# Splitting each store's 16 KB run per partition into two runs of 8 KB, in a per-sample 128x128 matmul with residual

## The chip, the cores and the metric

One NeuronCore of a Trainium2 chip runs the program. The metric is device microseconds of one execution, as the median of several executions. Inputs and outputs lie in HBM; all of x (67.1 MB) is read once and an output of the same size is written once.

## What is computed

There are 128 samples of x, each 128 channels by 1024 times in float32, eight weight matrices of 128x128, and an index per sample that names its matrix.

```
def reference(x, itok_B_0_7, L0_cond_weights):       # (128,128,1024) f32, (128,) int32, (8,128,128) f32
    w = weights[subjects]                            # subjects = itok_B_0_7
    out = jnp.einsum('bct,bcd->bdt', x, w)
    return x + out
```

## The kernel before, in words

**Tiling.** Four samples make a group (G = 2 samples to a pair, H = 2 pairs to a group), so there are NT = 32 groups. A group lives in one of SLOTS = 12 tiles in SBUF, `xs[k]`, of 128 partitions by 4 samples by 1024 floats: 16 KB in each partition, 2.1 MB in all. The result is added in place, so the same tile is loaded, computed on and stored from.

**Loads.** SyncE's queue (SP) issues all loads, in the order of the samples, one DMA for each sample (`load`, line 121). On the HBM side a sample is described as 16 pieces of 8 lines (`rearrange("(a r) t -> a (r t)", r=ROWS)`, ROWS = 8), each 32 KB without a gap; on the SBUF side as 128 partitions of 4 KB. Each of the 16 DMA engines takes one 32 KB piece and fills eight partitions with it. From the thirteenth group on SP first waits until the slot's former group has been stored (lines 165 to 167: `s_first` once, then `s_pair[k][H - 1]` at the count that `emptied` gives). So loads can run ahead of stores by twelve groups at most, 25.2 MB.

**Compute.** For each pair of samples GpSimd (POOL) copies the two weight matrices that the index names (line 196), waiting for the pair's load. TensorE multiplies (line 206, eight matmuls of 128x512 to a pair) into PSUM, and VectorE adds PSUM and the tile into the tile (line 217).

**Stores.** ScalarE's queue (ACT) issues the stores (`store`, line 130) as soon as VectorE is done with their samples (line 222). Groups 1 to 30 have one store each, of all four samples. Group 0 has two stores of two samples each. The last group has one of two samples and one of one sample, and the very last sample goes by an ordinary DMA at the end. On the HBM side a store is described as 128 lines (d) by so many samples (g) of 4 KB each; on the SBUF side, by line 136, as one run for each partition, 16 KB long where there are four samples, 8 KB where there are two. Each of the 16 DMA engines takes eight partitions.

Loads and stores thus stand on two queues, which the same 16 DMA engines serve. In the profile the queue of the loads is q1 and that of the stores q10. Each load or store also ends with one transfer of 4 bytes on every engine that counts up its semaphore; these stand in the profile's DMA records among the ones under 512 B.

Of the kernel before, what the change touches and what calls it, by code (L numbers as in the profile page):

```python
# [30 lines left out]
G = 2  # L31
# [18 lines left out]
def transfer(nc, engine, out, in_):  # L50

    later, nc._always_lower_symbolic_ap = nc._always_lower_symbolic_ap, False
    ins, outs = engine.lower_ap_dma(in_), engine.lower_ap_dma(out)
    nc._always_lower_symbolic_ap = later
    return engine.add_instruction(  # L57
        mybir.InstDMACopy(
            name=nc.get_next_instruction_name(),
            engine=engine.engine,  # L60
            ins=ins,
            outs=outs,
            mode="Copy",
            cce_op=ALU.bypass,
            queue=QUEUES[engine.engine],
        )
    )
# [3 lines left out]
def kernel(  # L71
# [12 lines left out]
    def sbuf(name, *shape, dtype=F32):  # L84
        return ctx.enter_context(nc.sbuf_tensor(name, list(shape), dtype)).ap()
# [7 lines left out]
    xs = [sbuf(f"x{i}", C, H * G, T) for i in range(SLOTS)]  # L93
# [36 lines left out]
    def store(i, q0, q1):  # L130
        k, b = i % SLOTS, i * H * G
        transfer(
            nc,
            nc.scalar,
            out[b + q0 : b + q1].rearrange("g d t -> d g t"),
            xs[k][:, q0:q1, :].rearrange("d (o g) t -> d o (g t)", o=1),
        ).then_inc(s_first if i == 0 and q1 == G else s_pair[k][(q1 - 1) // G], DMA)

    with tc.tile_critical():  # L139
# [22 lines left out]
        for i in range(NT):  # L162
            k = i % SLOTS
# [8 lines left out]
        for j in range(NT * H):  # L172
            i, q0, q1 = j // H, j % H * G, (j % H + 1) * G
            k = i % SLOTS
# [46 lines left out]
            if i == 0 or q1 == H * G or i == NT - 1:  # L221
                nc.scalar.wait_ge(s_added, j + 1)
                store(i, q0 if i in (0, NT - 1) else 0, q1 - (b == B - 1))
# [42 lines left out]
```

## Time and profile before

| what | value |
|---|---|
| median of three runs (lowest to highest) | 347.12 us (345.59 to 358.03) |
| the profiled execution | 345.59 us, span 343.8 us |
| TensorE matmul busy | 243.7 us, 71% of the span |
| VectorE busy | 147.8 us, 43% |
| GpSimd busy | 34.0 us, 10% |
| read from HBM, written to HBM | 67.63 MB, 67.11 MB |
| mean rate over the span | 392 GB/s |
| loads (q1): share of the 16 DMA engines' span | 51.4% |
| stores (q10): the same | 46.7% |

The span is the time from the first to the last instruction that the profile shows; 1.8 us of the execution's own time lie around it. In the profile's DMA tables a queue's row gives its packets, the MB that they moved and the time that they took, as a share of 16 engines' time in the stretch that was asked for. So a share of 50% in a stretch of 10 us is 80 us of DMA engine time. Tables by stretch count the span from its start.

### The profile page before, as it was taken

Reading aid. Unit: us, or ns where it says so; the run is one execution under the profiler, and the core shown is the slowest. Engines: PE = TensorE matmul, PEld = TensorE weight load, DVE = VectorE, ACT = ScalarE, POOL = GpSimd, SP = SyncE. Lnnn points to the kernel's source line nnn. Section 1 sums busy time; section 2 is a strip of 40 time slices with the busy share of each in tenths; the row PEclk is TensorE's granted clock in tenths of the full one; section 3 lists DMA queues with packets and bytes.
Section 4 is the critical chain, followed back from the end, with each engine's and each line's share of the span. In section 5 each row is a group of like instructions: output and inputs, shape, how many; then the busy total and the mean of one; then the engine's idle time right before and its main releaser. Section 6 shows DMA issues by size and latency. Waiting matters only on the chain.

```text
span 343.8 us, 1606 instructions
## 1 busy us (share of the span) xinstructions
PE 243.7 (71%) x518; PEld 94.5 (27%) x518; DVE 147.8 (43%) x68; POOL 34.0 (10%) x132
## 2 busy tenths in 40 slices
PE   6886866877777887777887777887777877775000
PEld 2332322333222333222333232233322322231000
DVE  1164353445544445544445554445553455345000
POOL 1011011011111011111011111101111011010000
PEclk9899999999999999999999999999999999999555
DMA  7999999999999999999999999999999999999993
GB/s 198 236 260 296 283 356 425 417 431 426 423 425 427 427 427 427 417 426 425 431 421 425 431 422 429 423 411 410 417 416 414 404 416 419 429 410 427 427 420 132
DMA packets 10186, 134.85 MB, mean 392 GB/s; under 512 B 2625, under 2 KB 3650, under 8 KB 3906
## 3 DMA queue, kind: packets, MB, share of 16 engines
q1 hardware_dynamic: 5136, 67.64, 51.4%
q10 hardware_dynamic: 5042, 67.11, 46.7%
q8 instruction: 4, 0.07, 0.1%
q14 instruction: 4, 0.03, 0.0%
HBM read 67.63 MB, written 67.11 MB: 392 GB/s over the span
## 4 chain that ended last, share of the span: by engine, by line
PE 36%; issue 26%; DVE 21%; POOL 4%; DMA 2%; POOLq 1%; SPq 0%
PE ps L206 36%; DVE x L217 21%; POOL w L196 4%; DMA x<-in_x_dram 2%; POOLq L196 1%; POOLq L185 1%; SPq L57 0%; SPq L161 0%; POOLq L139 0%; SPq L262 0%; SPq L139 0%
## 5 line engine op out<-in xcount | busy, mean ns | idle before, releaser
L206 PE MATMUL ps<-x,w 128*128 128x512 f32 x512 | 238.3, 609 | 69.3 <-POOL w L196 66.2
L217 DVE TENSOR_TENSOR x<-ps,x 128x2048 f32<-128x2048 f32 x64 | 146.6, 2291 | 167.4 <-PE ps L206 167.4
L206 PEld LDWEIGHTS ps<-x,w 128*128 128x128 f32 x512 | 92.7, 191 | 215.6 <-POOL w L196 117.5
L196 POOL COPY w<-w_all 128x128 f32 x128 | 33.8, 293 | 276.7 <-DMA x<-in_x_dram 271.2
L146 PE MATMUL ps<-zeros 128*128 128x512 f32 x6 | 5.5, 1084 | 1.7 <-DVE zeros L143 1.7
L146 PEld LDWEIGHTS ps<-zeros 128*128 128x128 f32 x6 | 1.8, 326 | 3.8 <-issue 2.1
L143 DVE MEMSET zeros<- 128x512 f32 x1 | 0.5, 485 | 1.1 <-SPq L139 1.1
L153 DVE TENSOR_SCALAR near<-given 1x128 int32<-1x128 int32 x1 | 0.2, 216 | 0.6 <-DMA given<-in_itok_B_dram 0.6
L157 DVE CUSTOM_DVE_ANT_0 index<-near,wrap 1x256 uint16<-1x256 uint16 x1 | 0.3, 278 | 0.0
L155 DVE TENSOR_SCALAR wrap<-near 1x128 int32<-1x128 int32 x1 | 0.2, 215 | 0.0
L253 POOL MEMSET const-float32-0.0<- 128x1 f32 x1 | 0.1, 98 | 0.2 <-issue 0.2
L253 POOL MEMSET const-bfloat16-1.0<- 128x1 bf16 x1 | 0.1, 101 | 0.0
L253 POOL MEMSET const-uint8-127<- 128x1 uint8 x1 | 0.1, 101 | 0.0
L253 POOL MEMSET const-float32-1.0<- 128x1 f32 x1 | 0.1, 98 | 0.0
## 6 DMA issues: line engine op xcount, KB each, us to landing
x<-in_x_dram SPq DMA_DIRECT2D x128, 512.0 KB, 36.5
out_dram<-x ACTq DMA_DIRECT2D x30, 2048.0 KB, 40.0
out_dram<-x ACTq DMA_DIRECT2D x3, 1024.0 KB, 25.7
out_dram<-x ACTq DMA_DIRECT2D x2, 512.0 KB, 21.2
w_all<-in_L_cond_weights_dram SPq DMA_DIRECT2D x1, 512.0 KB, 4.8
given<-in_itok_B_dram ACTq DMA_DIRECT2D x1, 0.5 KB
```

The costliest lines, as they stand in the source:

```text
L143: nc.vector.memset(zeros, 0.0).then_inc(s_zeros, 1)
L146: nc.tensor.matmul(ps[P_SLOTS - 1][:, G - 1, :N], zeros[:, :D], zeros, start=True, stop=True)
L153: nc.vector.tensor_scalar(near, given, -S, S - 1, ALU.max, ALU.min).then_inc(s_index, 1)
L155: nc.vector.tensor_scalar(wrap, near, 0, S, ALU.is_lt, ALU.mult).then_inc(s_index, 1)
L157: nc.vector.tensor_tensor(index, near, wrap, ALU.add).then_inc(s_index, 1)
L185: _, subject = nc.values_load_multi_w_load_instructions(index[0:1, b : b + R], engines=[mybir.EngineType.Pool], min_val=0, max_val=S - 1, ...
L196: copy = nc.gpsimd.tensor_copy(ws[b % W_SLOTS], w_all[:, bass.ds(subject[b % R], 1), :])
L206: mm = nc.tensor.matmul(p[:, q % G, t : t + N], ws[(i * H * G + q) % W_SLOTS][:, 0, :], xs[k][:, q, t : t + N], start=True, stop=True,)
L217: nc.vector.tensor_tensor(mine, p, mine, ALU.add).then_inc(s_added, 1)
L253: nc = _bacc.Bacc("TRN2", target_bir_lowering=False, num_devices=1)
```

## The change

One line of `store` changes, in how the SBUF side of a store is described. With four samples, a partition's 16 KB are now two runs of 8 KB (two samples each), where they were one run of 16 KB. For stores of two samples `min(G, q1 - q0)` is 2 and for one of one sample it is 1, which gives one run as before: the stores of groups 0 and 31 stay as they were. The bytes, the HBM side, the loads, the order on every queue and all semaphores are the same.

```
--- before.py
+++ after.py
@@ -133,7 +133,7 @@
             nc,
             nc.scalar,
             out[b + q0 : b + q1].rearrange("g d t -> d g t"),
-            xs[k][:, q0:q1, :].rearrange("d (o g) t -> d o (g t)", o=1),
+            xs[k][:, q0:q1, :].rearrange("d (o g) t -> d o (g t)", g=min(G, q1 - q0)),
         ).then_inc(s_first if i == 0 and q1 == G else s_pair[k][(q1 - 1) // G], DMA)
 
     with tc.tile_critical():
```

More of the change, by code (lines that the diff above doesn't have):

```diff
@@ L135, in store @@
             out[b + q0 : b + q1].rearrange("g d t -> d g t"),
-            xs[k][:, q0:q1, :].rearrange("d (o g) t -> d o (g t)", o=1),
+            xs[k][:, q0:q1, :].rearrange("d (o g) t -> d o (g t)", g=min(G, q1 - q0)),
         ).then_inc(s_first if i == 0 and q1 == G else s_pair[k][(q1 - 1) // G], DMA)
```

## The prediction

> **What bounds the kernel now.** I read the page's busy slices first. The lines are the mean busy share of the 16 DMA engines and what they moved, in 40 slices of 8.6 us; below them the row of GpSimd's weight copies, whose idle time says what compute waits for.
>
> ```profile
> DMA  7999999999999999999999999999999999999993
> GB/s 198 236 260 296 283 356 425 417 431 426 423 425 427 427 427 427 417 426 425 431 421 425 431 422 429 423 411 410 417 416 414 404 416 419 429 410 427 427 420 132
> ...
> L196 POOL COPY w<-w_all 128x128 f32 x128 | 33.8, 293 | 276.7 <-DMA x<-in_x_dram 271.2
> ```
>
> The DMA engines are busy from end to end, and compute waits 271.2 us for loads: the kernel is bound by its transfers. But busy engines don't always move the same. In the first five slices they are as busy as later and move 198 to 296 GB/s, where later they move about 425. So I asked for four stretches (busy time of PE, PEld, DVE, POOL, then granted clock, DMA share, GB/s):
>
> ```profile
> 8.00:24.00 16.00, 12.53 (x24) 4.98 (x24) 5.05 (x3) 0.84 (x4) 0.89 1.00 234
> 28.00:44.00 16.00, 11.10 (x24) 4.31 (x24) 7.72 (x4) 1.59 (x6) 1.00 1.00 301
> 60.00:300.00 240.00, 188.55 (x408) 73.25 (x408) 115.95 (x51) 26.47 (x100) 1.00 1.01 422
> 312.00:335.00 23.00, 2.71 (x7) 0.93 (x5) 2.90 (x2) 0.00 (x0) 0.63 1.00 424
> ```
>
> Loads alone (8 to 24 us) run at 234 GB/s and stores alone (312 to 335) at 424. From 28 to 44 us loads run beside the two stores of group 0, which are already in runs of 8 KB: 301 GB/s. The first 16 KB run stands in the trace's transfer records at 46 us, and from there on the rate is 422. So the trace of before holds a stretch of what the change makes of the rest. The DMA queues' rows (packets, MB, share of 16 engines) of 28 to 44, of 60 to 300, of 335 to 338, of 0 to 46 and of 306 to 344 us, in this order:
>
> ```profile
> q1 hardware_dynamic: 201, 3.31, 72.1%
> q10 hardware_dynamic: 200, 1.51, 28.3%
> ...
> q1 hardware_dynamic: 3265, 53.52, 53.4%
> q10 hardware_dynamic: 3265, 47.58, 47.0%
> ...
> q10 hardware_dynamic: 192, 0.89, 71.9%
> ...
> q1 hardware_dynamic: 1596, 9.90, 82.9%
> q10 hardware_dynamic: 284, 2.10, 13.9%
> ...
> q10 hardware_dynamic: 1218, 13.40, 83.4%
> ```
>
> Look at the MB. From 60 to 300 us loads and stores stand as 53.52 to 47.58, which is 1.125. From 28 to 44 they stand as 2.19. And both queues have the same number of packets in both stretches. That is what turns taken one transfer at a time give. A load is two transfers on each engine (32 KB and its semaphore). A store of four samples is nine (eight of 16 KB and its semaphore), so nine turns against 4.5 loads: 4.5 x 32 / (8 x 16) = 1.125. With group 0's runs of 8 KB it is 4.5 x 32 / (8 x 8) = 2.25.
>
> What a load costs also differs. From 28 to 44 us, 72.1% of 256 us of engine time over 3.31 MB is 1828 ns for 32 KB, and a run of 8 KB costs 393 ns. From 60 to 300 it is 1256 ns, and a run of 16 KB costs 621 ns.
>
> **What the change does.** *More pieces.* Thirty stores have 256 runs in place of 128: 7680 of 8 KB for 3840 of 16 KB. Stores alone cost 618 ns for 16 KB (23 us x 16 engines over 9.76 MB) and 318 ns for 8 KB (71.9% of 48 us over 0.89 MB, with some of 4 KB in it). So 9 ns more a piece at most, 9 x 7680 / 16 = 4 us; nothing at least. I take 2.
>
> *Turns.* A store now takes 17 turns against 8.5 loads: loads to stores are 8.5 x 32 / (16 x 8) = 2.125, so of all bytes 68% are loads and 32% stores, as long as both queues hold work. Whether they do is the next step. A load lands 36.5 us (median) after its issue, some 8 MB at the 223 GB/s of loads from 60 to 300 us, so its queue is deep. And among the waits of SP the only ones of note for stores are those of line 229, at the program's end; the slot waits of lines 165 and 167 don't stand there. First the page's row of issues, then the row of SP's waits (total, times, longest):
>
> ```profile
> x<-in_x_dram SPq DMA_DIRECT2D x128, 512.0 KB, 36.5
> ```
>
> ```profile
> SPq L229 <- DMA out_dram<-x: 18.3, 3, 9.8
> ```
>
> So slots are no limit now. With 68 to 32 they become one. Three stages follow.
>
> *Stage 1, from 46 us until twelve slots are full.* At 46 us 9.90 MB less 0.52 of weights are loaded, 9.38, and 2.10 stored: 7.3 MB in slots, of 25.2. I take the rate from the row that has this mix, 301 GB/s. Loads gain 36% of it on stores, 108 GB/s, so the other 17.9 MB fill in 165 us: to 211 us. By then 43.2 MB are loaded and 18.0 stored; before, that stretch ran at 421.
>
> *Stage 2, loads held by slots.* The load queue runs empty, a store ends, and SP issues one group's loads to all engines at once. The 23.9 MB left to load go one for one with stores, 47.8 MB. How fast, no row says directly. If the one-to-one mean decides, it is 422 GB/s as from 60 to 300: 113 us. If each burst goes as from 28 to 44, an engine needs 4 x (1828 + 2 x 393) + 8 x 318 = 13,000 ns for its share of 4.19 MB, 323 GB/s: 148 us. Half of the runs go beside loads, half don't, so I take the middle, 372 GB/s: 128 us, to 339 us.
>
> *Stage 3, stores alone.* 67.1 - 18.0 - 23.9 = 25.2 MB at 424 GB/s are 59 us, and the tail stays: 37.8 us from 306 on less 13.40 MB at 424 leave 6 us.
>
> Sum: 211 + 128 + 59 + 6 + 2 = 406, and 1.8 outside the span: 408, against the profiled execution's 345.6 (the median of the runs, 347.1, is 0.4% above). With stage 2's ends: 393 to 428.
>
> Compute is no cover and no cost: in the chain of waits TensorE's eight matmuls of a pair take 3.71 us, and pairs will come more slowly. ACT issues as many DMAs as before; if more pieces hold it, only later stores stand behind, and those wait for engines anyway. SP's waits on slots, nearly free now, become long, with nothing behind them but loads that have no room.
>
> **Two rules beside the rows.** The trace's turns are of one transfer, by the 1.125 and 2.19. The Trainium skill (DMA: Bandwidth & Descriptors, Queues, rings and completion order) says that an engine drains a whole packet, about 9 to 17 descriptors typically, before it switches. By that both halves of a run could stay in one turn and the time would be about 347. And loads alone move 234 GB/s here. The same page (Bandwidth, Measured) has 425 GB/s for a 16 MB load; with that, a mix with more loads would cost nothing, again about 347. The rows of this case speak against both.
>
> **Rivals.** *Only reading is capped.* The 301 GB/s could be a start-up of the mix, while the true limit is the 234 GB/s that loads reach alone. Then stage 1 runs at 234 / 0.68 = 344, fills 17.9 MB at 124 in 144 us, to 190 us; stage 2 takes 113 us at full rate, or 131 with bursts at 2240 ns a load (4 x 2240 + 8 x 318). With 59, 6, 2 and 1.8: 372 to 390. For it: a plain limit. Against: from 28 to 44 us loads moved only 3.31 MB / 16 us = 207.
>
> *Not slower: the first 46 us are slow for their own sake.* Loads may be slow early because all engines start in step, or for the place of the first samples, and the 8 KB runs are there by chance. Then a load keeps its 1256 ns, stage 1 runs near 421, loads only get ahead, stores alone end it at 424, and 2 us are added: 347.6, 345 to 350. It decides if 32 KB beside two runs of 8 KB moves at full rate, which asks reads of 0.68 x 421 = 286 GB/s; from 60 to 300 they were 223. For it: nothing else differs so sharply in time as start and rest. Against: the change of rate falls on the first 16 KB runs.
>
> *The change does nothing.* The two runs adjoin in SBUF and could be merged into 16 KB again: 346. Against it: the built program describes the side as 128 x 2 x 2048 floats.
>
> Faster is hardly to be had: from 46 us on all bytes move at 421 of 424.
>
> **The numbers.** The three stages at mixed rates: 52%, 393 to 428, at 408. Reading capped: 24%, 372 to 390. Slow start only: 18%; merged: 3%. Something that I don't see makes it faster: 3%. A measurement here tells about 2% from no change. So faster 0.03, same 0.21, slower 0.76. Leaving out the no-change cases would leave out more than 2 in 10, so the range runs from 346 to 428; that of the likeliest case is 393 to 428.
>
> **What would show it.** About twice the packets of over 4 KB on q10; loads to stores near 2.1 in MB and near 300 GB/s from 46 to about 210 us; SP held on stores from then on; the last load landing well before the end, with nearly 60 us of stores alone. Wrong if the rate from 60 us on is again 420 (slow start), or the packets are as many as now (merged).

## The result, and the profile after

| | before | changed |
|---|---|---|
| median, us (six executions each) | 357.18 (345.59 to 360.32) | 399.84 (383.28 to 415.60) |
| ratio | | 1.1075, 95% interval 1.0963 to 1.1186 |
| the profiled execution, us | 345.59 (span 343.8) | 383.88 (span 382.1) |
| transfers on the stores' queue (q10) | 5042 | 8882 |
| last load landed, us of the span | 309 | 328 |

The change makes the kernel 11% slower. Executions of both kernels scatter by 4 to 8%, so the ratio is taken from the quickest ones of each (383.28 and 383.88 us against 345.59 and 347.12); what goes with the scatter comes out below.

The page of the changed kernel shows the busy share of the DMA engines and what they moved in 40 slices (now of 9.6 us), the two queues, and how long a load takes from issue to landing:

```profile
DMA  9999999999999999999999999999999999999996
GB/s 220 220 248 281 301 305 295 300 302 316 334 402 421 424 423 425 410 347 356 318 295 366 346 413 314 362 362 352 386 357 411 372 407 357 385 427 426 425 425 281
...
q1 hardware_dynamic: 5136, 67.64, 54.7%
q10 hardware_dynamic: 8882, 67.11, 44.6%
...
x<-in_x_dram SPq DMA_DIRECT2D x128, 512.0 KB, 15.9
```

The DMA engines are as busy as before, but after the start, where loads stand alone, four stretches follow each other: some 300 GB/s up to about 95 us, then 420 to 425 up to about 155, then an uneven stretch of 295 to 413, then 425 with stores alone. The same four, asked for as stretches (columns: busy time of PE, PEld, DVE, POOL, granted clock, DMA share, GB/s):

```profile
46.00:90.00 44.00, 31.81 (x67) 12.48 (x66) 18.54 (x9) 4.24 (x16) 0.96 1.01 302
110.00:155.00 45.00, 44.59 (x99) 17.62 (x98) 27.90 (x13) 6.88 (x26) 1.00 1.01 423
165.00:330.00 165.00, 115.39 (x224) 46.49 (x224) 64.15 (x28) 15.26 (x58) 0.87 1.01 359
335.00:370.00 35.00, 0.00 (x0) 0.00 (x0) 1.80 (x1) 0.00 (x0) 0.53 1.01 426
```

The queues' rows for 46 to 90 us, for 110 to 155 and for 340 to 370:

```profile
q1 hardware_dynamic: 551, 8.98, 70.9%
q10 hardware_dynamic: 553, 4.27, 29.6%
...
q1 hardware_dynamic: 788, 12.94, 68.4%
q10 hardware_dynamic: 787, 6.06, 32.4%
...
q10 hardware_dynamic: 1664, 12.80, 101.4%
```

Loads to stores are 8.98 to 4.27 = 2.10 and 12.94 to 6.06 = 2.14, with equal numbers of transfers on both queues. So the mix is the same in both stretches, and yet one runs at 302 and the other at 423 GB/s. Per 32 KB piece of a load that is 70.9% of 704 us of engine time over 274 pieces, 1.82 us, against 68.4% of 720 us over 395, 1.25 us. SP's waits for slots show that these were full. The row is what SP waited for at the loads' line, in total, times, longest:

```profile
SPq L57 <- DMA out_dram<-x: 155.2, 16, 14.3
```

Before, there was no such row. That a load now lands 15.9 us after its issue and not 36.5 says the same: its queue is often empty.

### The profile page after: what moved, and what is told of

The parts are those of the page before. It is cut to its first block, busy times and chain, and to the rows that moved or that the text cites. A ratio compares the mean times of both kernels' runs of the same rounds, so it can differ in the third digit from the quotient of the medians.

```text
span 382.1 us, 1606 instructions
## 1 busy us (share of the span) xinstructions
PE 256.4 (67%) x518; PEld 102.4 (27%) x518; DVE 147.8 (39%) x68; POOL 34.0 (9%) x132
## 3 DMA queue, kind: packets, MB, share of 16 engines
q10 hardware_dynamic: 8882, 67.11, 44.6%
## 4 chain that ended last, share of the span: by engine, by line
PE 46%; issue 23%; DVE 13%; POOL 3%; DMA 2%; POOLq 1%; SPq 0%
PE ps L206 46%; DVE x L217 13%; POOL w L196 3%; DMA x<-in_x_dram 2%; POOLq L196 1%; SPq L57 0%; SPq L161 0%; POOLq L185 0%; SPq L262 0%; SPq L139 0%
## 5 line engine op out<-in xcount | busy, mean ns | idle before, releaser
L206 PE MATMUL ps<-x,w 128*128 128x512 f32 x512 | 251.5, 643 | 76.4 <-POOL w L196 72.1
L206 PEld LDWEIGHTS ps<-x,w 128*128 128x128 f32 x512 | 100.5, 205 | 227.5 <-POOL w L196 116.7
## 6 DMA issues: line engine op xcount, KB each, us to landing
x<-in_x_dram SPq DMA_DIRECT2D x128, 512.0 KB, 15.9
```

Of the source, the lines that this page charges most:

```text
L206: mm = nc.tensor.matmul(p[:, q % G, t : t + N], ws[(i * H * G + q) % W_SLOTS][:, 0, :], xs[k][:, q, t : t + N], start=True, stop=True,)
```

## The experiments

The prediction took 301 GB/s for a property of the mix. The trace of the changed kernel already speaks against that. From there two theories stood: **A**, runs of 8 KB beside loads are slow in themselves, and something else ended it; **B**, slowness belongs to the 32 KB loads when they stand alone, and a mix heavy in loads keeps it where an even mix ends it. Each experiment is one profiled execution unless a median is given. With 32 KB loads two executions of one kernel can lie 20 to 32 us apart, so what follows rests on the rates within one execution, and a single span is rough.

### 1. The same mix after another start

```
-            xs[k][:, q0:q1, :].rearrange("d (o g) t -> d o (g t)", g=min(G, q1 - q0)),
+            xs[k][:, q0:q1, :].rearrange("d (o g) t -> d o (g t)", g=(q1 - q0) if i <= 3 else min(G, q1 - q0)),
```

> Runs of 16 KB for groups 0 to 3 as in the kernel before, 8 KB from group 4 on. Theory A (8 KB runs beside loads always give about 300 GB/s): 420 GB/s from about 46 to 76 us, then about 300 until the slots are full; span near 400 us. Theory B (the slow state stems from the start, where loads stand alone; a mix of 8 KB runs only fails to end it): 420 GB/s goes on after 76 us with loads to stores near 2.1, until the slots are full at about 190 us, then about 370; span near 357 us.

Span 362.4 us. Stretches of this kernel:

```profile
28.00:44.00 16.00, 12.03 (x27) 4.76 (x28) 8.33 (x4) 1.60 (x6) 1.00 1.03 310
60.00:80.00 20.00, 16.76 (x34) 6.71 (x35) 8.66 (x4) 2.13 (x8) 0.91 1.00 420
85.00:170.00 85.00, 84.78 (x188) 33.69 (x187) 53.12 (x24) 12.27 (x46) 1.00 1.01 423
190.00:310.00 120.00, 86.79 (x170) 34.77 (x169) 48.13 (x21) 11.21 (x42) 0.87 1.01 359
```

From 85 to 170 us the runs are of 8 KB again, and the queues' rows for this stretch give 24.35 to 11.54 MB, 2.11: the mix of the slow stretch, at 423 GB/s for 85 us. Theory A falls. Three groups of 16 KB runs end the slow loads (60 to 80 us), and 8 KB runs don't bring it back. The bursts at the end (359) stay.

### 2. Runs of 16 KB where the slots are full

```
-            xs[k][:, q0:q1, :].rearrange("d (o g) t -> d o (g t)", g=min(G, q1 - q0)),
+            xs[k][:, q0:q1, :].rearrange("d (o g) t -> d o (g t)", g=(q1 - q0) if i >= 8 else min(G, q1 - q0)),
```

> Runs of 8 KB for groups 1 to 7, 16 KB from group 8 on, which meets full slots. If the second stage's loss stems from turns (loads 2.1 to 1, so they come in bursts), it is gone: about 420 GB/s from the end of the first stage (some 165 to 210 us) on, span near 360 us. If it stems from full slots as such, about 370 GB/s stays and the span is near 380 us.

Span 384.2 us:

```profile
46.00:120.00 74.00, 52.63 (x115) 20.51 (x114) 32.43 (x15) 7.41 (x28) 1.00 1.00 292
...
210.00:330.00 120.00, 86.09 (x179) 33.57 (x177) 50.42 (x22) 11.65 (x44) 0.96 1.00 384
```

The expectation that turns make the second stage slow missed: with nearly even turns and full slots the rate is 384, somewhat over the 359 of 8 KB runs but far from 420. By its span this is the rival's case, full slots as such; experiment 6 shows that it isn't that either. The first, slow stretch, whose runs are those of the changed kernel, lasted longer here, to about 129 us: its length differs from execution to execution.

### 3. Loads alone, in pieces of 32, 16 and 4 KB

Three kernels that load all of x and leave out compute and all stores but the last sample's, the first with ROWS = 8 and then

```
-ROWS = 8
+ROWS = 4
```

and ROWS = 1 in the third.

> Leaves out compute and all stores but the last sample: the loads of x alone, in 32 KB pieces, each group waiting for its slot's former load. If loads alone are slow by themselves: 234 GB/s to the end, span near 295 us. If slow for the start of the program only: rate rises to about 425 after some 50 to 100 us, span near 190 to 220 us.

> The same, but each sample is read as 128 pieces of 4 KB, one to a partition. If the 32 KB piece makes loads slow: well above 234 GB/s, 350 to 425, span 165 to 200 us. If reading by 16 engines at these addresses is slow in any pieces: 234 again, span near 295 us.

> As the run of loads alone (compute and all stores but the last sample left out), with 64 pieces of 16 KB a sample in place of 32 KB (231 GB/s) and 4 KB (410 GB/s). If loads slow down with the piece's size gradually: between, 300 to 380 GB/s, span 185 to 230 us. If only pieces over 16 KB are slow: about 410 to 425, span near 170 us.

Stretches within the steady part, columns: length, busy time of POOL, granted clock, DMA share, GB/s. First 32 KB:

```profile
20.00:280.00 260.00, 0.00 (x0) 1.00 1.01 235
```

then 16 KB:

```profile
20.00:150.00 130.00, 0.00 (x0) 1.00 1.01 409
```

and 4 KB:

```profile
20.00:150.00 130.00, 0.00 (x0) 1.00 1.03 410
```

The spans are 296.0, 173.6 and 173.5 us. It is neither the program's start nor reading by 16 engines as such: the same bytes into the same partitions move at 409 or 410 GB/s in pieces of 16 or 4 KB and at 235 in pieces of 32 KB, to the end. Of the two cases written down for 16 KB the second holds: the loss comes in one step between 16 and 32 KB. ROWS sets more than the size, though. A load gives each engine one piece of 32 KB, two of 16 KB or eight of 4 KB, and a piece fills eight, four or one partitions. No run keeps these apart, for instance by giving each engine two pieces of 32 KB in one load; "pieces of 32 KB" below stands for loads cut in this way.

### 4. Loads alone, 32 KB after a fast start

```
-            x[i * H * G + q].rearrange("(a r) t -> a (r t)", r=ROWS),
+            x[i * H * G + q].rearrange("(a r) t -> a (r t)", r=1 if i < 4 else ROWS),
```

> Loads alone (compute and all stores but the last sample left out), 4 KB pieces for groups 0 to 3, 32 KB from then on. If 32 KB pieces are slow only where all engines start them together: over 400 GB/s throughout, span near 172 us. If they are slow where they stand alone: 410 GB/s for 8 MB, then about 231; span near 280 us.

```profile
8.00:20.00 12.00, 0.00 (x0) 1.00 1.03 413
30.00:250.00 220.00, 0.00 (x0) 1.00 1.01 240
```

Span 275.1 us. So 32 KB loads that stand alone are slow even when they follow a fast stretch. It isn't the common start of all engines.

### 5. The changed kernel and the kernel before with that fast start

The same edit of `load`, in the changed kernel:

> The changed kernel with the loads of groups 0 to 3 in 4 KB pieces, 32 KB from group 4 on. If the slow state stems from 32 KB pieces that stand alone at the start: about 410 GB/s from some 5 us on and no stretch near 300 before the slots are full; then bursts at about 370; span 335 to 350 us. If 32 KB pieces beside 8 KB runs fall into it by themselves: about 300 GB/s from group 4's loads (some 25 us) on, span 370 us or more.

Span 355.4 us:

```profile
46.00:140.00 94.00, 92.21 (x205) 36.66 (x203) 58.17 (x26) 13.68 (x52) 1.00 1.01 421
155.00:290.00 135.00, 90.70 (x181) 35.92 (x182) 52.60 (x23) 11.64 (x44) 0.90 1.00 341
```

The 32 KB loads meet stores from their first moment on and run at 421 GB/s, at a mix of 26.91 to 12.63 MB, 2.13. What is left is the second stage, at 341. The same in the kernel before, timed:

> The kernel before with the same start: groups 0 to 3 in 4 KB pieces. The first 46 us of before move 12 MB, which at 410 GB/s take 29 us after a start of 4: if the slow start is just this, 13 us less than before, ratio near 0.965. If the loads that come sooner only wait for compute and slots, ratio 0.99 to 1.0.

Median 341.90 us (341.31 to 350.09, five executions) beside 357.11 (342.79 to 361.92, seven). The profiled one took 347.94:

```profile
8.00:30.00 22.00, 21.81 (x51) 9.62 (x52) 12.36 (x6) 2.67 (x10) 1.00 1.03 420
36.00:54.00 18.00, 15.07 (x25) 6.28 (x26) 4.69 (x3) 2.13 (x8) 0.74 0.98 340
...
310.00:346.00 36.00, 11.10 (x24) 4.31 (x24) 8.11 (x4) 1.12 (x5) 0.76 0.53 222
```

The medians differ by 15 us, but the quickest executions don't: three of the five took 341.31 to 341.90, the quickest of the seven 342.79. So no gain is shown over a quick execution of the kernel before. The profiled one, among the longer of the five, shows where time went in it. By 46 us it has moved 16.98 MB where the kernel before moved 11.99. The first 32 KB loads begin at 35 us, and from 36 to 54 the rate is 340, though stores of 16 KB runs stand beside them. At the end the DMA engines are busy for only 53% and move 222 GB/s: the last load lands at 318 us and not at 309, and the last stores wait for compute. Whether the quick executions end in the same way no trace shows.

### 6. Small pieces only for the loads that meet full slots

```
-            x[i * H * G + q].rearrange("(a r) t -> a (r t)", r=ROWS),
+            x[i * H * G + q].rearrange("(a r) t -> a (r t)", r=ROWS if i < SLOTS else 4),
```

> The changed kernel with 32 KB pieces for the loads of groups 0 to 11 and 16 KB from group 12 on, whose loads are the ones that meet full slots. If the bursts of the second stage are slow for their 32 KB pieces: first stage near 300 GB/s for the 25 MB of 32 KB loads, then about 424 to the end; span about 355 to 362 us. If full slots as such cost: about 370 GB/s in the second stage, span near 380 us.

Span 349.7 us:

```profile
28.00:44.00 16.00, 11.33 (x25) 4.54 (x26) 7.81 (x4) 1.82 (x7) 1.00 0.99 296
...
120.00:160.00 40.00, 34.58 (x76) 13.51 (x75) 21.03 (x10) 4.76 (x18) 1.00 1.01 425
200.00:300.00 100.00, 80.51 (x168) 32.04 (x166) 47.06 (x21) 10.59 (x40) 0.95 1.01 425
```

With 16 KB pieces the second stage runs at 425 GB/s. The slots are full all the same: SP waited 127.1 us for stores here. So full slots cost nothing by themselves; bursts of 32 KB pieces do.

Curing the second stage takes 382.1 - 349.7 = 32.4 us off the changed kernel's span, curing the start 382.1 - 355.4 = 26.7, together 59.1; curing both (next) takes 57.5. That these agree so well may be chance, since the spans are single executions, three of them of kernels with 32 KB pieces; the rates (425 for 359, 421 for 302) are the firmer evidence.

### 7. All loads in 16 KB pieces

```
-ROWS = 8
+ROWS = 4
```

In the changed kernel, first a single execution, then six, and in the kernel before:

> The changed kernel with loads in 16 KB pieces. A load then takes three turns, a store 17: loads to stores 17/3 x 32 / 128 = 1.42 where both queues are full, so slots fill more slowly. If the loss of the changed kernel stems from its 32 KB pieces beside 8 KB runs: no stretch near 300 GB/s, about 420 from some 25 us on, span 325 to 345 us. If 8 KB runs slow any load: about 300 to 340 GB/s until the slots are full, span over 370 us.

> The changed kernel with loads in 16 KB pieces, timed. If its one look (326.3 us) holds: ratio to the kernel before 0.91 to 0.95. If that look was a lucky one: ratio within 2% of 1.

> The kernel before with loads in 16 KB pieces, stores in runs of 16 KB. If the load's piece alone decides: no slow start, about 424 GB/s from some 12 us on, span near 325 us, as with 8 KB runs (within 2 us). If the run of 8 KB has a worth of its own: more than 1% slower than the changed kernel with such loads. A load then has three turns to a store's nine, loads to stores 0.75, so that loads can fall short of compute: some us more.

| runs of the stores | loads | median, us | range |
|---|---|---|---|
| 16 KB | 32 KB (the kernel before) | 355.19 | 339.98 to 360.78, 11 executions |
| 8 KB | 16 KB | 326.64 | 326.25 to 327.29, 6 |
| 16 KB | 16 KB | 327.95 | 327.55 to 328.12, 6 |

The single execution of the changed kernel with 16 KB loads, span 324.6 us, and then its queues from 60 to 130 us:

```profile
8.00:24.00 16.00, 15.50 (x36) 6.94 (x37) 8.34 (x4) 1.60 (x6) 1.00 1.02 416
28.00:44.00 16.00, 15.37 (x37) 6.29 (x35) 10.01 (x6) 2.67 (x10) 1.00 1.00 422
60.00:200.00 140.00, 123.33 (x267) 47.65 (x266) 75.63 (x33) 17.75 (x67) 1.00 1.01 425
200.00:300.00 100.00, 64.13 (x137) 25.17 (x136) 41.26 (x18) 8.95 (x34) 0.87 1.01 425
```

```profile
q1 hardware_dynamic: 1597, 17.40, 58.9%
q10 hardware_dynamic: 1597, 12.30, 41.9%
```

No stretch is slow, whether loads stand alone, beside two groups' stores or in bursts. Turns still set the mix: 17.40 to 12.30 is 1.41, and 17 turns of a store against three of a load give 1.42. In the kernel before with such loads, the 0.75 that was expected from nine turns against three did not come about: from 60 to 280 us loads moved 46.86 MB and stores 46.60. A store landed 13.2 us (median) after its issue there, where the changed kernel with 16 KB loads has 46.5, so its queue was often empty, and turns set the mix only while both queues hold work. The 8 KB run, which cost 11% beside 32 KB loads, costs nothing here: it is 1.3 us quicker (0.4%, the ranges don't meet). The slowest of these six executions (327.29) is 3.7% under the quickest of the eleven of the kernel before. And the scatter is gone: 1.0 us from end to end, against 20.8.

## Why the prediction was right, and where it wasn't

It forecast 408 us and slower; the median is 399.84, and the profiled execution, against which the sum was made, took 383.9. The direction and the reason, turns that fill the slots, were right. That the time came so near is partly luck. The quick executions (383.28 and 383.88) lie below the 393 to 428 of the case that was held likeliest and inside the 372 to 390 of a rival that the runs refute. And the terms were off in opposite directions: stage 1 took 46 us less than forecast, stage 2 35 us more, the rest 13 us less.

**Turns.** Right. It said 2.125 to 1, and 2.10 and 2.14 were measured; experiment 7 repeats it at another ratio. The rule of the Trainium skill that was weighed there (DMA: Bandwidth & Descriptors, Queues, rings and completion order), a whole packet of some 9 to 17 descriptors before an engine switches, is not what these queues show. By it, nine or more transfers of one queue would follow each other on an engine. The transfer records name no engine, but a transfer starts 3 to 8 ns before the record of its forerunner ends, so they can be put in chains. From 110 to 155 us of the changed kernel the next transfer in the chain is the other queue's in 1550 of 1575 cases: a load's 32 KB, a run of 8 KB, the load's 4 bytes, a run of 8 KB, and so on.

**More pieces.** 2 us were taken, of 0 to 4. Stores alone cost 101.4% of 480 us over 12.80 MB, 312 ns for 8 KB, against 309 for half of 16 KB: 3 x 7680 / 16 = 1.4 us at most.

**Stage 1, the step that failed: "I take the rate from the row that has this mix, 301 GB/s".** The row was right for as long as it held (302 from 46 to 90 us), but it wasn't a property of the mix. The stretch ended by itself near 100 us and went on at 423 with the same mix. The trace of before held the missing half of the reading: in its first row, loads alone at 234, the pieces are those 32 KB, and the prediction weighed that only as a limit on all reading. Experiment 3 puts it down to how the loads are cut. "Faster is hardly to be had" failed for the same reason: the sentence looked from 46 us on, and with 16 KB loads the kernel before moves 414 GB/s from 8 to 24 us and takes 327.95 us, 12 us under its quickest execution with 32 KB.

**When slots are full.** The prediction let stage 1 end with 25.2 MB in slots, at 211 us. At 165 us the changed kernel had loaded 38.3 MB and stored 15.9: 22.4 MB. A slot counts as taken from the issue of its load to the landing of its last store, so I read the missing 2.8 MB as loads and stores under way. Together with the faster second half of the stage that made it 46 us shorter.

**Stage 2.** Bursts were foreseen, and the middle of 372 GB/s; 359 were measured, over more bytes (58.4 MB from 165 to 328 us, for 47.8), so 163 us for 128. The reason given was incomplete. It isn't that half of the runs stand beside loads: with 16 KB runs the stage ran at 384, with 16 KB loads at 425. In a burst 32 KB loads come to all engines at once. In the transfer records from 165 to 328 us, 432 of 880 pieces of 32 KB took 1.65 us or more, as from 46 to 90 us, and 228 took under 1.35 us, as from 110 to 155: the stage goes back and forth between the two.

**Stage 3 and the tail** were 54 us for the predicted 59 and 6 (and 2 for the pieces), as 21.65 MB were left and not 25.2.

Sum: 165 + 163 + 54 = 382 where 211 + 128 + 67 = 406 stood.

**The rivals.** *Reading capped at 234 GB/s* falls: from 110 to 155 us the loads, beside stores, moved 12.94 MB, 288 GB/s, and experiment 3 has 410. *Slow for the start's own sake* was half right. The mix can run at full rate, and the 286 GB/s of reads that it asked for were reached. But with 32 KB pieces the slow loads outlasted the 46 us of the start by some 40 (experiment 6) to 85 us (experiment 2), and bursts brought it back. The change of rate at the first 16 KB runs, which I held against this rival, was real: the even mix of 16 KB runs ended the slow loads within some 20 us in the kernel before and in experiment 1. *Merged runs* fall with 3840 more transfers. The other rule weighed, 425 GB/s for a 16 MB load on the same page (Bandwidth, Measured; there for loads that GpSimd issues, here SyncE does), is near what 16 and 4 KB pieces gave here (409, 410) and not what 32 KB pieces gave (235).

**What stays open.** Why 32 KB pieces move at 235 GB/s where they stand alone and at full rate beside enough stores wasn't found, nor whether it is their size or that an engine gets one to a load; nor what ends the slow loads in a mix of 2.1 to 1 (near 100 us in the changed kernel, 129 in experiment 2). The records show only how long each transfer took. That this random end makes the executions scatter is argued from the stretches' lengths; what is shown is that the scatter is gone when the 32 KB pieces are.

## What to carry to other kernels

Two queues on the same engines share them by transfers, not by bytes, so cutting the pieces on one side hands the engines to the other; work out the mix from the turns and ask which buffer fills next. A busy DMA engine isn't a full-rate one: compare GB/s between stretches with the same busy share, and measure each stream alone before a rate is taken for a property of the mix. Here the way the loads are cut, which nobody changed, was the fault: with 16 KB pieces the change is harmless, and the kernel takes 326.64 us, 13 us less than the quickest execution of the kernel before and 28.5 less than its median.

## What the runs showed of the hardware that wasn't expected

- Loads alone: 235 GB/s in pieces of 32 KB, 409 in 16 KB, 410 in 4 KB, with the DMA engines fully busy in all three.
- One and the same mix of 32 KB loads and 8 KB runs (2.1 to 1 by bytes) ran at 302 and at 423 GB/s in one execution, and at 423 for 85 us after three groups of 16 KB runs.
- A 32 KB piece of a load took 1.82 us in the one stretch and 1.25 in the other.
